# Mamba and attention on four images: another order of work after the last tile of the last image

## The chip, the cores and the metric

The kernel runs on one core of one Trainium2 chip. The metric is the device time of one execution in microseconds (us); lower is better. Three runs of the kernel before gave 7833.92, 7839.31 and 7841.01 us, so the time before is the median, 7839.31 us. All data is float32 unless said.

## What is computed

The input `x` is (4, 512, 64, 64): four images of 512 channels and 4096 positions. Two layers follow each other, each behind a group norm over 16 channels, and each added to its own input:

```python
x = x + L0(_gn(x), ...)
x = x + L1(_gn(x), ...)

# L0: layer norm, a mamba on each of 4 chunks of 128 channels, layer norm, projection
xn = layer_norm(xf, norm_g, norm_b)
ym = mamba(chunks, ...) + skip_scale * chunks      # conv, silu, state scan over 4096 steps
y = einsum('blc,oc->blo', layer_norm(y, norm_g, norm_b), proj_w) + proj_b

# L1: linear attention with 8 heads of 64
q = relu(qkv[:, :, 0]); k = relu(qkv[:, :, 1]); v = qkv[:, :, 2]
kq = einsum('bnhc,bnhd->bhcd', k, q)
attn = einsum('bnhc,bhcd->bnhd', v, kq) / (kq.sum(axis=2) + EPS)
out = attn @ w_out.T + b_out
```

The second group norm needs the whole of an image's L0 output, and `kq` is a sum over all 4096 positions of an image. So the attention of an image can begin only when its last tile has left L0, and the output of L1 only when the whole `kq` is there.

## The kernel before

**Tiles and steps.** An image is cut into 8 tiles of 512 positions (`T`), a tile into 4 chunks of 128 channels. `steps` lists the 128 triples (image, tile, chunk). Each step has 16 slots. A slot scans two blocks of the state (L755, VectorE); ScalarE makes their decay by `Exp` straight into PSUM (L729), GpSimd makes their drive (L737, three buffers tagged `bx`), and every second slot the states are multiplied (VectorE L775 for 384 positions, GpSimd L767 for 128) and folded by TensorE into `y`. The states `h` have two buffers.

**What fills the gaps.** Inside `tc.manual_schedule()` (L1114 to L1202) instructions are issued in the order in which the code calls them. Everything else, the norms of the next tile, `projected` for the tile that has left, and the attention of the image before, is written as generators; `after()` lets them go on by one piece in a slot, `later(n, what)` puts a closure n slots off, `work_bank` takes one of three PSUM banks. `now[0]` is the slot; it is `None` ahead of the loop and behind it, and then nothing waits for a slot and all pieces run at once. Outside the manual part the framework places instructions itself; it may put one of the code behind the loop between instructions of the loop, at a place in its engine's queue where it takes the engine to be free.

**The prologue** (L1089 to L1112): the statistics of image 0, `tile_norm` of its first tile through `group_norm` (L374, ScalarE, four chunks) and `layer_norm` (L435 and L421: VectorE on all four chunks at once; squares at L443, scale at L454 on ScalarE), then the inputs of the first two steps.

**Behind the loop** (L1204 to L1210), for image 3 alone:

- the last chunk's gate and output projection `po`, copied into `xn` (L808);
- `projected` (L517): `layer_scale` sums the channels (`mu_sums`) and squares (L484, `var_sums`), takes mean and variance through two matmuls, and multiplies the tile by the root (L414, L415, L421); then 16 products `pp` with `w_pr`, `xr` by ScalarE (L527), and a GpSimd DMA that adds `x` from DRAM (L545); `shifted` sums values and squares on ScalarE (L575, tiles tagged `res`, two buffers); the tile goes out to DRAM (L548);
- `shifted_end` (L581) and `stats_end` (L344): the group norm's scale `gr` and offset `off` of the whole image;
- `attention` (L822): per 128 positions v, two sums `pq` (q and k) of a bias matmul `bqk` (bf16, L887) and four products with `w_qk`, a `relu` by ScalarE (L848), and 8 small products `pk` for `kq`, summed by VectorE (L855). The tile `xa` is normed on ScalarE (L374). Then `kq` over its norm (`kqn`: memset L912, GpSimd L915 and L919), `m2` (L929) and `m3` (L946), the offsets `pob` (32 products with one column, L967), the identity added to `m3` by GpSimd (L992), and for each tile 16 products `pr` with `m3`, stored by ScalarE and SyncE (L996, L998).

```python
   912          nc.gpsimd.memset(kqn, 0.0)
   ...
   992              nc.gpsimd.tensor_tensor(v, v, fold[r, :].unsqueeze(1).to_broadcast([BLK, NC, BLK]), ALU.add)
```

Of the kernel before, what the change touches and what calls it, by code (L numbers as in the profile page):

```python
# [24 lines left out]
def kernel(  # L25
# [343 lines left out]
    def group_norm(dst, xt, norm):  # L369
        gr, off, _ = norm  # L370
        for c in range(NC):
            if c % 2 == 0:
                yield from clear()
            nc.scalar.activation(  # L374
                dst[:, c, :], xt[:, c, :], AF.Identity,
                bias=off[:, c : c + 1], scale=gr[:, c : c + 1],
            )
            if c == 1:
                yield "free"
        yield  # L380
# [12 lines left out]
    def mean_of(sums, what, when, stop=True):  # L393
# [13 lines left out]
        mm(bank, mean.to_broadcast([P, P]), got, start=True, stop=stop)  # L407
        return bank

    def over_deviation(v, var, name):  # L410
        rs = wk.tile([P, T], F32, tag="sq", name=f"rs_{name}", bufs=4)

        def root():
            nc.scalar.activation(rs, var, AF.Ln, bias=eps)  # L414
            nc.scalar.activation(var, rs, AF.Exp, scale=-0.5)  # L415

        rooted = later(1, root)
        yield
        yield from until(rooted)
        yield "wide"  # L420
        nc.vector.tensor_tensor(v, v, bc(var, NC), ALU.mult)  # L421
        free()
        norming.clear()
        yield

    def layer_norm(v, name):
# [8 lines left out]
        nc.vector.tensor_tensor(v, v, bc(mu, NC), ALU.subtract)  # L435
        free()
        yield "free"
        sqs = []
# [111 lines left out]

    def shifted_stats(b):
# [27 lines left out]
    def shifted_end(f, name):  # L581
        mv = small.tile([P, NC, 2], F32, tag="mv", name=f"mv_{name}", bufs=4)
        for v in range(2):
            nc.vector.tensor_reduce(mv[:, :, v], f[("sum", "square")[v]], AX.X, ALU.add)
        nc.gpsimd.tensor_scalar(mv, mv, 1.0 / L, None, ALU.mult)
        d2 = small.tile([P, NC], F32, tag="d2", name=f"d2_{name}")
        nc.gpsimd.tensor_tensor(d2, mv[:, :, 0], mv[:, :, 0], ALU.mult)
        nc.gpsimd.tensor_tensor(mv[:, :, 1], mv[:, :, 1], d2, ALU.subtract)
        nc.gpsimd.tensor_tensor(mv[:, :, 0], mv[:, :, 0], f["mv"][:, :, 0], ALU.add)
        return mv  # L590


# [229 lines left out]
    def attention(b, x1s, stats):  # L822
# [2 lines left out]
        both = wk.tile([P, NC, C], F32, tag="m3", name=f"kq_{b}", bufs=1)  # L825
        kq = both[:, 0, 0 : C // 2].rearrange("p (c d) -> p c d", c=NC)
        tiles = {}

        def fetch(t, why, spare=1):

# [14 lines left out]
        qk, ready = {}, {}  # L845

        def relu(i, pq):
            nc.scalar.activation(qk[i], pq, AF.Relu)  # L848
            free()

        def add(pk, first):
            if first:
# [24 lines left out]
        for v in range(NT * SUB):  # L877
            t, u = divmod(v, SUB)
            if u == 0:
                gn = yield from fetched(t, "a")  # L880
                yield "free"
                yield from group_norm(gn, gn, norm)
            for j in range(2):
                yield from room()
                i = 2 * v + j
                pq = work_bank(f"pq_{b}_{i}")
                mm(pq, sel[:, 0, j * BLK : j * BLK + 1].to_broadcast([P, P]), bqk, start=True, stop=False)  # L887
                for c in range(NC):
                    mm(
                        pq, gn[:, c, u * P : (u + 1) * P], w_qk[:, c, j * C : (j + 1) * C],  # L890
                        start=False, stop=(c == NC - 1),
                    )
# [19 lines left out]
        nc.gpsimd.memset(kqn, 0.0)  # L912
        nrm = small.tile([P, NC], F32, tag="nrm", name=f"nrm_{b}")
        nc.vector.tensor_reduce(nrm, kq, AX.X, ALU.add)
        nc.gpsimd.tensor_scalar(nrm, nrm, 1e-6, None, ALU.add)  # L915
        nc.vector.reciprocal(nrm, nrm)
        for i in range(P // HEAD):
            r = slice(i * HEAD, (i + 1) * HEAD)
            nc.gpsimd.tensor_tensor(  # L919
                kqn[r, :, r], kq[r, :, :],  # L920
                nrm[r, :].unsqueeze(2).to_broadcast([HEAD, NC, HEAD]), ALU.mult,
            )
# [3 lines left out]
        taken = []  # L926

        def take2(p, pm):
            nc.scalar.copy(m2[:, p, :], pm)  # L929
            free()  # L930

        for p in range(NC):
# [12 lines left out]
        def take3(m, pm):  # L945
            nc.scalar.activation(m3[:, m, :], pm, AF.Copy, scale=gr[:, m : m + 1])  # L946
            free()

        for m in range(NC):
            yield from room()  # L950
# [19 lines left out]
        for o in range(NC):  # L970
            yield from room()
            pm = work_bank(f"pob_{b}_{o}")
            for p in range(NC):
# [11 lines left out]
        yield from until(*taken)  # L985
        free_x()
        free_x()
        for k in range(P // BLK):
# [59 lines left out]
    def leave(b, t):  # L1048
# [4 lines left out]
                for i in range(NT)  # L1053
            ]
        ym = xn[b, t][:, :, NTAP - 1 : NTAP - 1 + T]
        yield from projected(ym, stats1[b], x1s[b][t], b, t)
        if t == NT - 1:
            add_to(rest, attention(b, x1s[b], stats1[b]))

# [204 lines left out]
```

## Time and profile before

| | us |
|---|---|
| median of the runs | 7839.31 |
| the profiled execution | 7841.1 |
| its span, first to last instruction | 7839.4 |
| first scan of the loop starts | 120.77 |
| last scan of the loop ends | 7363.56 |
| first product `pq` of image 3 with `w_qk` | 7426.73 |
| first product `pr` of image 3 | 7722.29 |

| engine | busy us | share of the span |
|---|---|---|
| TensorE (PE) | 6444.4 | 82% |
| VectorE (DVE) | 6905.7 | 88% |
| ScalarE (ACT) | 5461.7 | 70% |
| GpSimd (POOL) | 6898.4 | 88% |

The page gives the busy share of each engine in 40 slices of the span, the chain of work that ended last, and the costliest groups of instructions with what ended the idle time ahead of them. The timeline lists instructions with start and length; equal ones that follow each other are merged ("x8"), and a bracket tells idle time and its releaser. PEld is TensorE's weight load, SPq the queue of SyncE. A float32 matmul stands in the trace as two instructions. All helpers that call `mm` have the line L129, so matmuls are told apart by their tiles. Mean granted TensorE clock: 0.905.

### The profile page before, as it was taken

Reading aid. Unit: us, or ns where it says so; the run is one execution under the profiler, and the core shown is the slowest. Engines: PE = TensorE matmul, PEld = TensorE weight load, DVE = VectorE, ACT = ScalarE, POOL = GpSimd, SP = SyncE. Lnnn points to the kernel's source line nnn. Section 1 sums busy time; section 2 is a strip of 40 time slices with the busy share of each in tenths; the row PEclk is TensorE's granted clock in tenths of the full one; section 3 lists DMA queues with packets and bytes.
Section 4 is the critical chain, followed back from the end, with each engine's and each line's share of the span. In section 5 each row is a group of like instructions: output and inputs, shape, how many; then the busy total and the mean of one; then the engine's idle time right before and its main releaser. Section 6 shows DMA issues by size and latency. Waiting matters only on the chain.

```text
span 7839.4 us, 90421 instructions
## 1 busy us (share of the span) xinstructions
PE 6444.4 (82%) x24839; PEld 2099.0 (27%) x24880; DVE 6905.7 (88%) x5650; ACT 5461.7 (70%) x8329; POOL 6898.4 (88%) x4649
## 2 busy tenths in 40 slices
PE   5677777677789888988788888898788888989599
PEld 1121212112223222322222223332222222323144
DVE  5999999999999999999999999999999999999500
ACT  4677777777777777777777777777777777777421
POOL 4999999999999999999999999999999999999500
PEclk7888878888899999998899999999899999999799
DMA  5666666666666656776666666676666666586302
GB/s 164 165 172 168 158 150 162 162 157 169 174 179 169 159 159 159 192 197 169 174 166 169 167 162 160 171 190 183 164 160 168 157 162 154 148 212 182 100 33 91
DMA packets 829184, 1265.87 MB, mean 161 GB/s; under 512 B 183912, under 2 KB 317560, under 8 KB 816384
## 3 DMA queue, kind: packets, MB, share of 16 engines
q1 hardware_dynamic: 804736, 1222.32, 59.6%
q0 software_dynamic: 16896, 33.56, 2.5%
q8 instruction: 195, 3.19, 0.2%
q10 hardware_dynamic: 7040, 4.20, 0.2%
q14 instruction: 317, 2.60, 0.1%
HBM read 1052.78 MB, written 206.57 MB: 161 GB/s over the span
## 4 chain that ended last, share of the span: by engine, by line
DVE 33%; PE 31%; ACT 10%; issue 8%; DMA 7%; POOL 7%; SPq 3%; POOLq 0%; DVEq 0%; ACTq 0%
DVE h L755 21%; DVE h L775 10%; PE pq L129 6%; PE y L129 6%; PE pc L129 5%; POOL bx L737 5%; ACT dA L729 4%; DMA d_all<-d_rows 3%; PE pr L129 3%; PE po L129 2%; SPq L704 2%; PE pp L129 2%; DMA c_sb<-c_rows 2%; PE pd L129 1%; DMA b_all<-b_rows 1%
## 5 line engine op out<-in xcount | busy, mean ns | idle before, releaser
L737 POOL TENSOR_TENSOR bx<-d_all,b_all 128x1024 f32<-128x1024 f32 x2048 | 4824.0, 2367 | 198.2 <-DVE h L755 178.6
L755 DVE TENSOR_TENSOR_SCAN h<-dA,st,bx 128x512 f32<-128x512 f32 x3584 | 4355.5, 1265 | 292.5 <-PE y L129 101.8
L729 ACT ACTIVATE dA<-d_all,a_t 128x512 f32<-128x512 f32 x4096 | 2759.0, 688 | 1491.5 <-DVE h L755 1434.8
L775 DVE TENSOR_TENSOR h<-h,c_all 128x1536 f32<-128x1536 f32 x1024 | 1768.6, 1727 | 0.1
L767 POOL TENSOR_TENSOR h<-h,c_sb 128x512 f32<-128x512 f32 x1024 | 1299.8, 1269 | 99.1 <-DMA c_sb<-c_rows 13.0
L129 PE MATMUL y<-h,fold 128*32 128x512 f32 x8192 | 1264.0, 693 | 45.7 <-POOL h L767 42.4
L129 PE MATMUL c_all<-parts,sel 128*128 128x384 bf16 x1024 | 369.4, 361 | 1021.9 <-DVE h L775 1020.7
L129 PE MATMUL pc<-xn,w_cv 128*128 128x512 f32 x2048 | 1036.6, 639 | 126.0 <-DVE xn L421 62.2
L129 PE MATMUL pq<-w_qk,xa 128*128 128x512 f32 x2048 | 962.5, 602 | 6.7 <-issue 4.1
L755 DVE TENSOR_TENSOR_SCAN h<-dA,bx 128x512 f32<-128x512 f32 x512 | 590.1, 1204 | 76.6 <-ACT dA L729 46.5
L129 PEld LDWEIGHTS pc<-xn,w_cv 128*128 128x128 f32 x2048 | 386.4, 199 | 735.6 <-issue 409.3
L129 PEld LDWEIGHTS <-sel 128*128 128x128 bf16 x1280 | 126.8, 99 | 1668.0 <-DVE h L775 1453.4
L129 PEld LDWEIGHTS pq<-w_qk,xa 128*128 128x128 f32 x2048 | 395.7, 195 | 437.4 <-issue 421.7
L129 PE MATMUL pp<-xn,w_pr 128*128 128x512 f32 x1024 | 478.0, 597 | 3.8 <-DVE xn L421 3.8
L129 PE MATMUL pr<-xb,m 128*128 128x512 f32 x1024 | 476.1, 603 | 4.8 <-POOL m L992 2.2
L129 PE MATMUL y<-xz,dg 32*32 32x512 f32 x2048 | 362.1, 785 | 0.0
L129 PEld LDWEIGHTS y<-h,fold 128*32 128x32 f32 x8192 | 170.5, 114 | 639.7 <-issue 398.1
L848 ACT ACTIVATE kq<-pq 128x512 f32<-128x512 f32 x256 | 150.8, 589 | 265.5 <-PE pq L129 264.8
L797 POOL TENSOR_TENSOR xz<-xz 128x512 f32<-128x512 f32 x256 | 325.1, 1270 | 10.2 <-ACT xz L794 9.3
L644 POOL TENSOR_TENSOR dt<-dt,xz 128x1024 f32<-128x1024 f32 x128 | 302.1, 2360 | 21.4 <-ACT dt L636 21.4
L855 DVE TENSOR_TENSOR kq<-pk,kq 128x256 f32<-128x256 f32 x124 | 51.2, 413 | 277.9 <-PE pk L129 277.7
L129 PE MATMUL pd<-xz,w_xp 128*128 128x512 f32 x512 | 289.3, 692 | 5.2 <-ACT xz L1066 5.2
(178 smaller groups left out, 6164.7 us busy)
## 6 DMA issues: line engine op xcount, KB each, us to landing
d_all<-d_rows SPq DMA_DIRECT2D x2048, 256.0 KB, 4.3
b_all<-b_rows SPq DMA_DIRECT2D x4096, 64.0 KB, 2.3
d_rows<-dt SPq DMA_DIRECT2D x256, 512.0 KB, 2.7
c_sb<-c_rows SPq DMA_DIRECT2D x4096, 16.0 KB, 3.5
xs<-in_x_dram SPq DMA_DIRECT2D x32, 1024.0 KB, 7.8
xn<-in_x_dram SPq DMA_DIRECT2D x32, 1024.0 KB, 8.4
xr<-in_x_dram POOLq DMA_DIRECT2D x32, 1024.0 KB, 10.2
x<-xr SPq DMA_DIRECT2D x32, 1024.0 KB, 4.5
```

The lines of the kernel that those rows point to most:

```text
L129: nc.tensor.matmul(out_, lhsT, rhs, **how)
L644: nc.gpsimd.tensor_tensor(f["both"][:, 1], f["both"][:, 0], f["xz"][:, 0], ALU.mult)
L704: nc.sync.dma_start(dst[k * BLK : (k + 1) * BLK, :], rows_[q * KS + k, :].partition_broadcast(BLK))
L729: nc.scalar.activation(dAs[k], fs[n]["d_all", e][:, 0, j, :], AF.Exp, scale=a_t[:, e, j, q : q + 1])
L737: nc.gpsimd.tensor_tensor(bxs[g], fs[n]["d_all", e][:, 1, jj * 2 : jj * 2 + 2, :], bc(b_all[g // JJ], 2), ALU.mult)
L755: nc.vector.tensor_tensor_scan(h[:, j, :], dAs.pop(2 * g + i), bxs[g][:, i, :], 0.0 if t == 0 else st[:, c, e, q, j : j + 1], ALU.mult, AL ...
L767: nc.gpsimd.tensor_tensor(h[:, :, CUT:], h[:, :, CUT:], bc(c_sb.pop(g // JJ), NJ), ALU.mult)
L775: nc.vector.tensor_tensor(own, own, bc(c_all.pop(g // JJ), NJ), ALU.mult)
L797: nc.gpsimd.tensor_tensor(f["xz"][:, 1, e, :], f["xz"][:, 1, e, :], f["xz"][:, 0, e, :], ALU.mult)
L848: nc.scalar.activation(qk[i], pq, AF.Relu)
L855: nc.vector.tensor_tensor(kq, pk, kq, ALU.add)
```

## The change

Line numbers in this section are those of the diff's own code; L-numbers elsewhere are of the kernel before. Where `now[0]` is `None` (prologue and end) or the image is the last:

- `group_norm` does every second chunk on VectorE; `over` does the two layer norm operations of VectorE chunk by chunk instead of in one instruction.
- `projected_last` takes the place of `projected` for the last tile: the products `pp` are made of the tile before its norm, chunk by chunk into four banks of their own, and VectorE multiplies them by the root `rs` behind; `x` is loaded early by SyncE and added by VectorE; the statistics come from `bn_stats`.
- the small operations of `shifted_end` and of `kqn` go from GpSimd to VectorE.
- the last attention adds the q/k bias on VectorE to the sum in PSUM, with the bias loaded over all partitions into a `bx` buffer, and ScalarE then does `Relu` in place; the bias matmul goes.
- `m2` is copied by ScalarE and VectorE in turn; the identity is added by VectorE in 16 blocks as `m3` comes; `pob` is taken in four banks, first all products with `m2`, then those with `m3` (which has its identity by then, so `ngm` is taken off `bo` first).

```diff
@@ group_norm
+            if now[0] is None and c % 2:
+                nc.vector.tensor_scalar(
+                    dst[:, c, :], xt[:, c, :], gr[:, c : c + 1], off[:, c : c + 1], ALU.mult, ALU.add
+                )
+            else:
+                nc.scalar.activation(
+                    dst[:, c, :], xt[:, c, :], AF.Identity,
+                    bias=off[:, c : c + 1], scale=gr[:, c : c + 1],
+                )
...
+    def over(v, m, op):
+        if now[0] is None:
+            for c in range(NC):
+                nc.vector.tensor_tensor(v[:, c, :], v[:, c, :], m, op)
+        else:
+            nc.vector.tensor_tensor(v, v, bc(m, NC), op)
...
+    def projected_last(ym, f, x1, b, t):
+        nm = f"{b}_{t}"
+        xt = load_now(cols(x, b)[:, :, t * T : (t + 1) * T], f"xr_{nm}")
+        sq = wk.tile([P, NC, T], F32, tag="h", name=f"sq_{nm}", bufs=2)
+        sums, squares = work_bank(f"mu_sums_{nm}"), work_bank(f"var_sums_{nm}")
+        for c in range(NC):
+            nc.scalar.activation(sq[:, c, :], ym[:, c, :], AF.Square, bias=about)
+            sums_into(sums, {c: ym[:, c, :]}, (c,))
+            sums_into(squares, {c: sq[:, c, :]}, (c,))
+        got = {}
+        for what, bank in (("mu", sums), ("var", squares)):
+            got[what] = wk.tile([P, T], F32, tag="sq", name=f"got_{what}_{nm}", bufs=4)
+            nc.scalar.copy(got[what], bank)
+        mu = work_bank(f"mu_{nm}")
+        mm(mu, mean.to_broadcast([P, P]), got["mu"], start=True, stop=True)
+        mu2 = wk.tile([P, T], F32, tag="sq", name=f"mu2_{nm}", bufs=4)
+        nc.scalar.activation(mu2, mu, AF.Square, bias=about)
+        var = work_bank(f"var_{nm}")
+        mm(var, mean.to_broadcast([P, P]), got["var"], start=True, stop=False)
+        mm(var, minus_first.to_broadcast([P, P]), mu2, start=False, stop=True)
+        rs = wk.tile([P, T], F32, tag="sq", name=f"rs_{nm}", bufs=4)
+        nc.scalar.activation(rs, var, AF.Ln, bias=eps)
+        nc.scalar.activation(rs, rs, AF.Exp, scale=-0.5)
+        last = small.tile([P, NC, 1, 6], F32, tag="first", name=f"last_{nm}")
+        pps = [spare_bank(f"pp_{nm}_{o}", o) for o in range(NC)]
+        for c in range(NC):
+            for o in range(NC):
+                mm(
+                    pps[o], w_pr[:, c, o * P : (o + 1) * P], ym[:, c, :],
+                    start=(c == 0), stop=(c == NC - 1),
+                )
+        for o in range(NC):
+            nc.vector.tensor_tensor(sq[:, o, :], pps[o], rs, ALU.mult)
+            nc.vector.scalar_tensor_tensor(
+                xt[:, o, :], sq[:, o, :], pb[:, o : o + 1], xt[:, o, :], ALU.add, ALU.add
+            )
+            nc.vector.bn_stats(last[:, o, 0, :], xt[:, o, :])
+        nc.sync.dma_start(x1, xt)
+        mv = aggregate(last, f"last_{nm}")
...
+    def spare_bank(name, i):
+        if i < LEAD:
+            return ps_d.tile([P, T], F32, tag="dA", name=name)
+        return ps_y.tile([P, T], F32, tag="y", name=name)
...
@@ attention
+        last = b == B - 1
+        if last:
+            bias = wk.tile([P, 2, C], F32, tag="bx", name=f"bias_{b}", bufs=3)
+            nc.sync.dma_start(
+                bias.rearrange("p j c -> p (j c)"), b_qkv[0 : 2 * C].partition_broadcast(P)
+            )
...
         def relu(i, pq):
+            if last:
+                nc.vector.tensor_tensor(qk[i], pq, bias[:, i % 2, :], ALU.add)
+                free()
+                nc.scalar.activation(qk[i], qk[i], AF.Relu)
...
-                mm(pq, sel[:, 0, j * BLK : j * BLK + 1].to_broadcast([P, P]), bqk, start=True, stop=False)
+                if not last:
+                    mm(
+                        pq, sel[:, 0, j * BLK : j * BLK + 1].to_broadcast([P, P]), bqk,
+                        start=True, stop=False,
+                    )
...
         def take2(p, pm):
-            nc.scalar.copy(m2[:, p, :], pm)
+            if last and p % 2:
+                nc.vector.tensor_copy(m2[:, p, :], pm)
+            else:
+                nc.scalar.copy(m2[:, p, :], pm)
...
+            if last:
+                for k in range(P // BLK):
+                    r = slice(k * BLK, (k + 1) * BLK)
+                    v = m3[r, m, m * P + k * BLK : m * P + (k + 1) * BLK]
+                    nc.vector.tensor_tensor(v, v, fold[r, :], ALU.add)
...
+        if last:
+            banks = [spare_bank(f"pob_{b}_{o}", o) for o in range(NC)]
+            nc.vector.tensor_tensor(bo, bo, ngm, ALU.subtract)
+            for v, rhs in ((m2, bv), (m3, ngm)):
+                for o in range(NC):
+                    for p in range(NC):
+                        mm(
+                            banks[o][:, 0:1], v[:, p, o * P : (o + 1) * P], rhs[:, p : p + 1],
+                            start=(v is m2 and p == 0), stop=(v is m3 and p == NC - 1),
+                        )
...
-        yield from projected(ym, stats1[b], x1s[b][t], b, t)
+        do = projected_last if now[0] is None else projected
+        yield from do(ym, stats1[b], x1s[b][t], b, t)
```

More of the change, by code (lines that the diff above doesn't have):

```diff
@@ L373, in group_norm @@
                 yield from clear()
[L374 to L377, printed above, removed]
+            if now[0] is None and c % 2:
[7 more added lines that the diff above has]
+                )
             if c == 1:
@@ L420, in over_deviation @@
         yield "wide"
-        nc.vector.tensor_tensor(v, v, bc(var, NC), ALU.mult)
+        over(v, var, ALU.mult)
         free()
@@ L434, in layer_norm @@
         yield "wide"
-        nc.vector.tensor_tensor(v, v, bc(mu, NC), ALU.subtract)
+        over(v, mu, ALU.subtract)
         free()
@@ L549, in projected @@
         later(2, free_x)
+    def projected_last(ym, f, x1, b, t):
[37 more added lines that the diff above has]
+        mv = aggregate(last, f"last_{nm}")
+        d = mv[:, :, 0]
+        nc.vector.tensor_tensor(d, d, f["mv"][:, :, 0], ALU.subtract)
+        nc.vector.tensor_scalar(f["sum"][:, :, t], d, float(T), None, ALU.mult)
+        nc.vector.tensor_tensor(d, d, d, ALU.mult)
+        nc.vector.tensor_tensor(d, d, mv[:, :, 1], ALU.add)
+        nc.vector.tensor_scalar(f["square"][:, :, t], d, float(T), None, ALU.mult)
+        free_x()
+        yield
@@ L584, in shifted_end @@
             nc.vector.tensor_reduce(mv[:, :, v], f[("sum", "square")[v]], AX.X, ALU.add)
-        nc.gpsimd.tensor_scalar(mv, mv, 1.0 / L, None, ALU.mult)
+        eng = nc.vector if now[0] is None else nc.gpsimd
+        eng.tensor_scalar(mv, mv, 1.0 / L, None, ALU.mult)
         d2 = small.tile([P, NC], F32, tag="d2", name=f"d2_{name}")
-        nc.gpsimd.tensor_tensor(d2, mv[:, :, 0], mv[:, :, 0], ALU.mult)
-        nc.gpsimd.tensor_tensor(mv[:, :, 1], mv[:, :, 1], d2, ALU.subtract)
-        nc.gpsimd.tensor_tensor(mv[:, :, 0], mv[:, :, 0], f["mv"][:, :, 0], ALU.add)
+        eng.tensor_tensor(d2, mv[:, :, 0], mv[:, :, 0], ALU.mult)
+        eng.tensor_tensor(mv[:, :, 1], mv[:, :, 1], d2, ALU.subtract)
+        eng.tensor_tensor(mv[:, :, 0], mv[:, :, 0], f["mv"][:, :, 0], ALU.add)
         return mv
@@ L847, in relu @@
         def relu(i, pq):
-            nc.scalar.activation(qk[i], pq, AF.Relu)
-            free()
+            if last:
[3 more added lines that the diff above has]
+            else:
+                nc.scalar.activation(qk[i], pq, AF.Relu)
+                free()
         def add(pk, first):
@@ L890, in attention @@
                         pq, gn[:, c, u * P : (u + 1) * P], w_qk[:, c, j * C : (j + 1) * C],
-                        start=False, stop=(c == NC - 1),
+                        start=(last and c == 0), stop=(c == NC - 1),
                     )
@@ L914, in attention @@
         nc.vector.tensor_reduce(nrm, kq, AX.X, ALU.add)
-        nc.gpsimd.tensor_scalar(nrm, nrm, 1e-6, None, ALU.add)
+        eng = nc.vector if last else nc.gpsimd
+        eng.tensor_scalar(nrm, nrm, 1e-6, None, ALU.add)
         nc.vector.reciprocal(nrm, nrm)
@@ L918, in attention @@
             r = slice(i * HEAD, (i + 1) * HEAD)
-            nc.gpsimd.tensor_tensor(
+            eng.tensor_tensor(
                 kqn[r, :, r], kq[r, :, :],
@@ L928, in take2 @@
         def take2(p, pm):
-            nc.scalar.copy(m2[:, p, :], pm)
+            if last and p % 2:
+                nc.vector.tensor_copy(m2[:, p, :], pm)
+            else:
+                nc.scalar.copy(m2[:, p, :], pm)
             free()
@@ L968, in offset @@
             free()
-        for o in range(NC):
+        if last:
[8 more added lines that the diff above has]
+                        )
+            for o in range(NC):
+                offset(o, banks[o])
+        for o in range(0 if last else NC):
             yield from room()
@@ L987, in attention @@
         free_x()
-        for k in range(P // BLK):
+        for k in range(0 if last else P // BLK):
             r = slice(k * BLK, (k + 1) * BLK)
```

## The prediction

> **What bounds the kernel now.** I read the slices of the page first, then the chain of waits and the windows behind the loop, then the timeline at the places that the change touches.
>
> ```profile
> PE   5677777677789888988788888898788888989599
> ...
> DVE  5999999999999999999999999999999999999500
> ...
> POOL 4999999999999999999999999999999999999500
> ```
>
> Two regimes: up to slice 37 VectorE and GpSimd are both full; in the last three slices they are at rest and TensorE is full. The loop ends at 7363.56 us, so the end of image 3 is 476 us, 6% of the span. A wait or an instruction there is on the path unless TensorE covers it.
>
> ```profile
> 7406.63 8.36 DMA xr<-in_x_dram
> ...
> 7426.73 12.82 PE pq L129 x24
> ...
> 7688.85 20.04 PE pm L129 x40
> ...
> 7708.89 11.24 PE pob L129 x64
> ...
> 7722.29 113.10 PE pr L129 x256
> ```
>
> This is the chain in order of time: a serial head until 7426.73, then TensorE without a break but for a hand-over at 7684.5 and another at 7720.
>
> ```profile
> 7443.76 0.38 PE L129 MATMUL pq<-bqk,sel 128*128 128x512 bf16 x1
> ...
> 7443.98 3.60 PE L129 MATMUL pq<-w_qk,xa 128*128 128x512 f32 x8
> ```
>
> The bias matmul starts 0.22 us ahead of the next: its price on a full TensorE.
>
> ```profile
> 7277.15 0.19 POOL L766 COPY st<-h 128x4 f32<-128x4 f32 x1
> ...
> 7278.64 4.68 POOL L737 TENSOR_TENSOR bx<-d_all,b_all 128x1024 f32<-128x1024 f32 x2
> ...
> 7281.05 1.28 DVE L755 TENSOR_TENSOR_SCAN h<-dA,st,bx 128x512 f32<-128x512 f32 x1 [0.53 <-ACT sum L575]
> ...
> 7281.07 0.72 ACT L575 ACTIVATE square<-xr,moff 128x512 f32<-128x512 f32 x1
> ...
> 7420.17 0.52 POOL L912 MEMSET kqn<- 128x512 f32 x1 [12.23 <-ACT sum L575]
> ```
>
> These are taken from two stretches of the timeline. In the first GpSimd is never idle, and its first `bx` of that pair (7278.64 to 7281.01) is ready just as the scan at 7281.05 takes it: no lead at all. The last line shows the memset of `kqn`, waiting for a buffer of tag `res`.
>
> **The Trainium skill.** (1) "TensorE: Matmul & The Clock Gate", part 1: the array runs at half clock until about 3.4 us of unbroken work, and falls back after as long a rest. The windows agree: granted clock 0.51 from 7376.0 to 7383.6, 0.99 from 7393.5 to 7405.2; a float32 product of 512 columns takes 1.71 or 0.86 us. (2) Same page, back-to-back issue gap: N / 2.4 GHz + 2.5 ns, 216 ns for 512 columns; measured 0.22 us. (3) Same page, the queue-depth row: ScalarE, VectorE and GpSimd are strict FIFO. The memset above, 12.23 us idle ahead of it, is what a blocked queue looks like. (4) "VectorE: DVE Perf Modes", walkthrough: a float32 tensor_tensor makes one element per cycle at 0.96 GHz, a tensor_scalar in SBUF two. Here 413 ns for 256 elements (L855), 682 for 512 (L321), 481 for a tensor_scalar of 512 (L315).
>
> **The parts.** Times are on the clock of the profile before.
>
> *Prologue.* Chunks overlap now. Norm: ScalarE's last of four ends at 59.6; two on each engine end at 58.15, and the sums of the channels follow: -1.4. Mean: 2.29 us in one instruction and then four squares end 4.5 us after the start; in chunks (0.60 us pitch, squares 0.62) 3.4: -1.1. Root: the first product `pc` needs chunk 0 alone; 2.29 + 0.73 becomes 0.69 + 0.73: -1.6. Together -4.1. The sums' burst is shorter, so the small matmul behind it, at full clock before (1.12 us), may fall to half (2.07, as at 70.56): +0.6 taken. Everything to the first scan at 120.77 hangs on this chain. Sum -3.5, between -2.0 and -4.1.
>
> *The loop.* The built order of instructions is the same on VectorE, ScalarE (bar three squares behind its last decay) and SyncE (bar one early load, whose buffer is long free). On GpSimd one row moves: the memset of `kqn` now stands inside the loop, between the copy at 7277.15 and L767 at 7277.42. The buffer that it takes is freed by the last square of tile 6 (7281.07 to 7281.79, its accumulator read to 7281.9). So GpSimd stands still until 7281.9; memset 0.52, L767 1.27, first `bx` 2.36: ready at 7286.1 for a scan that came at 7281.05. Queued behind the memset are L767, both `bx` and the next copies; VectorE's scans wait for them. GpSimd has no idle time until 7326, VectorE's later stalls wait for folds that hang on its own products, so nothing is made up: +5.1. Bounds: 0, were the lead larger, and 5.9, all of the stall. Not below zero, as nothing is taken from the loop. The memset's place at 7420.17 lay beside other work, so moving it gains nothing.
>
> *Head, 7363.56 to 7426.73.* Before: `po` ends 7371.6, sums, mean, squares, variance, root, norm to 7389.4, 16 products to 7405.2, `x` 8.36 us, ScalarE's statistics to 7420.8, then 4.6 from `pm` to `pq`. After: sums and squares of chunks 0 to 2 and four of the 16 products go ahead of or between the steps of chunk 3. TensorE works unbroken from 7365.57; full clock took 4.4 us from 7389.43, so I take it from 7370.5.
> - Last fold 7367.5; `var_sums` of three chunks 1.9, `pp_1` 1.4: 7370.8. `po`'s second product, which would have started at 7369.54, stands behind these: 7371.8. ScalarE copies `xn`, 7372.4.
> - `pp_2`, `mu_sums`, `pp_3`, `var_sums` of chunk 3 at 0.86 each: 7375.2; two copies 7375.9; `pp_0`, mean and variance 7377.6; ScalarE's square of the mean 0.69 and the last term: 7378.7. Root `rs` 7380.1.
> - 11 products left: 7388.0; bank 0 is full at 7385.5. `rs` is not late.
> - VectorE: three operations per bank (multiply from PSUM, add of `pb` and `x`, bn_stats: nearest rows 682, 682, 677 ns, 0.60 pitch) x 4 = 7.2 from 7385.6, aggregates 0.3: 7393.1. 11 small ones at 0.19: 7395.5. Then 4.6 as before, and 0.2 for the new operation on `bo`: first `pq` 7400.3.
>
> Gain 26.4; I take -26.0. At half clock throughout it is near -18; with full clock at once near -28. The old DMA of 8.36 us goes; the new load of `x` lands long before 7385.6. `xa_2` can load only after the last store (7392.7 + 4.5 + 7.6 = 7404.8), and its norms stand ahead of the second bias add on VectorE; the first `pq` sum lasts to about 7406, so this is covered by 1 us, and 6 us before TensorE needs it.
>
> *q and k.* 64 bias matmuls go. Three of them lay in the wait of `pm` (7422.6 to 7424.6): nothing. 61 x 0.22 = -13.4. Put in: per sum a VectorE add from PSUM (between 413 ns for half the size and 0.69; 0.69 taken) and a `Relu` from SBUF (0.60 as from PSUM). Both lie beside TensorE: `pk` of one v comes after a further `pq` of 3.43 us, and the two need 1.4 with hops. Bounds: -7.3, if `pk`'s neighbour then shows its weight load (0.19 x 32), to -14.
>
> *Hand-over at 7684.5.* The add is on the path, +0.7; GpSimd's two `kqn` products (0.61 each) and `nrm` become VectorE's (0.34 pitch, from 413 ns at this size): -0.7. Sum 0, +-0.5. The split copies of `m2` gain nothing: the products run without a gap from 7688.85, and a copy is due only when its chunk's turn comes.
>
> *End.* `pob` has its 32 products as before. The identity's four GpSimd steps and their hops, 7720.13 to 7722.29, go beside `m3`'s products on VectorE (16 small ones, four after the last, while 16 `pob` products with `m2` keep TensorE busy): -2.2, between -1 and -3.
>
> Sum: -3.5 + 5.1 - 26.0 - 13.4 + 0 - 2.2 = -40.0. The profiled execution took 7841.1, so 7801.1; it lies 1.8 above the median of the runs, 7839.31, against which the forecast is 7799.3.
>
> **Rivals.**
> - *No stall in the loop* (the square comes earlier, or GpSimd's lead is larger than this one execution shows): 7799.3 - 5.1 = 7794.2. Against it stands the row at 7281.05. Chance 0.20.
> - *TensorE stays cold in the head*, since the short waits between its steps don't count as work: head -18, 7807. For it: clock 0.50 and 0.51 up to 7383.6 before, with 5.1 of 7.15 us busy. Chance 0.13.
> - *The bias matmul hid a weight load*: q and k -7.3, 7805.4. For it: the "issue" pieces of 0.16 us beside `pk`. Chance 0.07.
> - *VectorE's queue is blocked by a norm that waits for its tile* (slower): the two norms of `xa_3` stand in its queue ahead of the add of `pq_9`, and so of `pk_4`. The load may start when tile 0 is done and lands 7.6 us later; `pk_4` needs the add 2.4 us after that, and norms, add and `Relu` take about 2.3. Five tiles are in this place. Each us of lateness then stops TensorE for 1 us: at 16 us per load the whole gain is gone (40 / 5 = 8 beyond the 7.7), beyond 20 us it is slower by over 0.2%, say 7860. Against it: DMA share 0.09 in this stage, and 3.4 us in all that ScalarE waited for these loads before. Chance 0.05: 0.03 within 0.2%, 0.02 slower.
> - *The forecast*, 0.55: 7799.3, by itself 7794 to 7805.
>
> **The numbers.** 0.2% is 15.7 us, about what a measurement of this kernel tells from no change. All cases but the blocked queue gain over 32 us: faster 0.93, with 0.02 for several failures at once within 0.2%, same 0.05, slower 0.02. The range takes in the no-stall case with the better bounds of the head and the prologue, and the cold head: 7790 to 7811.
>
> **What would show it.** Right: first scan near 117; a GpSimd gap of about 4.7 us ahead of the memset inside the loop, some 84 us ahead of the last scan, and last scan near 7365 (-3.5 + 5.1); 37 us from the last scan to the first `pq`; 7.58 us per v; 2 us from `pob` to `pr` gone. Wrong: full clock later than 5 us into the head; TensorE idle between `pq` and `pk`; a last scan earlier than 7362.

## The result, and the profile after

The changed kernel takes 7797.76 us (median of 6 runs, 7791.69 to 7819.03), the kernel before 7840.16 us (6 runs, 7833.92 to 7846.71). The ratio is 0.9948, with a 95% interval of 0.9937 to 0.9959, so the gain of 0.5% is clear of the noise. The forecast was 7799.3 us.

The profiled executions can be set side by side in six stretches, cut at events that both traces have. Scans are counted from 0; scan 4040 is the eighth ahead of the place where the memset now stands. The six add up to the two spans, 7839.39 and 7797.01 us.

| stretch, us | before | after | difference | predicted |
|---|---|---|---|---|
| start to first scan | 120.77 | 116.95 | -3.82 | -3.5 |
| first scan to scan 4040 | 7146.06 | 7141.50 | -4.56 | 0 |
| scan 4040 to the end of the last scan | 96.73 | 102.76 | +6.03 | +5.1 |
| last scan to first `pq` | 63.17 | 35.53 | -27.64 | -26.0 |
| first `pq` to first `pm` (q, k, hand-over) | 262.12 | 252.50 | -9.62 | -13.4 |
| first `pm` to the end | 150.54 | 147.77 | -2.77 | -2.2 |
| sum | | | -42.38 | -40.0 |

The slices of the page of the changed kernel:

```profile
PE   5677777677789888987788889898788888899699
...
DVE  5999999999999999999999999999999999999720
...
POOL 4999999999999999999999999999999999999700
```

The loop is as full as it was. VectorE's last three slices show 7, 2, 0 where they showed 5, 0, 0: it now works beside TensorE in the end of image 3. TensorE is full in the last slices as before.

The timeline of the changed kernel around the memset, where the prediction expected a stop (start, length, engine, line; in brackets the idle time ahead and what ended it):

```profile
7268.70 0.20 POOL L835 COPY st<-h 128x4 f32<-128x4 f32 x1
...
7272.66 0.72 ACT L643 ACTIVATE square<-xr,moff 128x512 f32<-128x512 f32 x1
...
7273.53 0.53 POOL L996 MEMSET kqn<- 128x512 f32 x1 [4.63 <-ACT square L643]
...
7275.23 4.66 POOL L806 TENSOR_TENSOR bx<-d_all,b_all 128x1024 f32<-128x1024 f32 x2
...
7277.62 1.28 DVE L824 TENSOR_TENSOR_SCAN h<-dA,st,bx 128x512 f32<-128x512 f32 x1 [5.52 <-POOL bx L806]
```

This answers to the lines of GpSimd shown of before. Where the copy was followed 0.27 us later by L767, GpSimd now waits 4.63 us for the last square of tile 6, clears `kqn`, and only then makes the `bx` that VectorE's next scan needs. VectorE stands still for 5.52 us; before it was 0.53.

The chain of waits of the changed kernel in the head, in order of time (start, length, engine, tile, line):

```profile
7375.13 6.88 PE pp L129 x16
7382.13 0.70 DVE sq L599
...
7389.32 0.58 DVE last L603
7389.90 0.23 DVE mv_last L341 x2
...
7394.51 1.05 POOL gr_b L364
...
7396.74 3.78 PE pq L129 x4
```

The DMA of 8.36 us and ScalarE's sums are gone from it. VectorE's work on the four banks, 7.8 us from 7382.13 to 7389.90, has taken their place. The rest of the chain of the changed kernel:

```profile
7649.24 20.25 PE pm L129 x40
7669.48 9.30 PE pob L129 x56
7682.20 110.92 PE pr L129 x254
```

`pr` no longer waits for GpSimd behind `pob`; two of its instructions lie inside `pob` already, as the timeline of TensorE shows:

```profile
7678.65 2.06 PE L129 MATMUL pr<-xb,m 128*128 128x512 f32 x2
7680.49 1.71 PE L129 MATMUL pob<-ngm_b,m 128*128 128x1 f32 x8
```

In the q and k stage of the changed kernel (timeline of TensorE) there is no bias matmul between the sums:

```profile
7410.02 0.69 PE L129 MATMUL pk<-kq 128*64 128x64 f32 x16
7410.64 7.13 PE L129 MATMUL pq<-w_qk,xa 128*128 128x512 f32 x16
7417.70 0.69 PE L129 MATMUL pk<-kq 128*64 128x64 f32 x16
```

From one `pk` to the next it is 7.68 us, not 8.02 as before and not 7.58 as predicted.

The clock in the head is the last thing to compare. The figures of the kernel before, and then those of the changed one, between the same two times (busy time and number of instructions by engine, then the granted clock, the share of the DMA engines and GB/s):

```profile
7364.00:7382.00 18.00, 11.66 (x22) 2.14 (x22) 1.43 (x1) 4.99 (x8) 2.42 (x2) 0.50 0.00 0
```

```profile
7364.00:7382.00 18.00, 17.87 (x47) 6.43 (x41) 0.00 (x0) 5.07 (x8) 1.26 (x1) 1.00 0.00 0
```

Before, TensorE executed 22 matmul instructions here at half clock, with a third of the time idle; now 47 at full clock, almost without a gap.

### The profile page after: what moved, and what is told of

It reads as the page before. It is cut to its first block, busy times and chain, and to the rows that moved or that the text cites. A ratio compares the mean times of both kernels' runs of the same rounds, so it can differ in the third digit from the quotient of the medians.

```text
span 7797.0 us, 90419 instructions
## 1 busy us (share of the span) xinstructions
PE 6424.5 (82%) x24816; PEld 2092.9 (27%) x24816; DVE 6968.4 (89%) x5784; ACT 5442.5 (70%) x8289; POOL 6892.5 (88%) x4637
## 4 chain that ended last, share of the span: by engine, by line
DVE 34%; PE 30%; ACT 10%; DMA 9%; issue 8%; POOL 6%; SPq 3%; DVEq 0%; POOLq 0%; ACTq 0%
DVE h L824 21%; DVE h L844 10%; PE y L129 6%; PE pc L129 6%; PE pq L129 5%; POOL bx L806 5%; DMA d_all<-d_rows 4%; ACT dA L798 3%; PE pr L129 3%; PE po L129 3%; SPq L773 3%; DMA c_sb<-c_rows 2%; PE pp L129 2%; DVE xn L421 2%; PE c_all L129 1%
## 5 line engine op out<-in xcount | busy, mean ns | idle before, releaser
L129 PE MATMUL pz<-xn,w_z 128*128 128x512 f32 x512 | 270.5, 621 | 7.5 <-ACT xz L692 6.0
L129 PE MATMUL po<-xz,w_op 128*128 128x512 f32 x512 | 258.8, 628 | 5.2 <-POOL xz L866 5.0
```

The source lines that it names most:

```text
L129: nc.tensor.matmul(out_, lhsT, rhs, **how)
```

## The experiments

Three questions were open: whether the memset is what costs 6 us and the 4.6 us gained ahead of it are chance; which parts the head's gain comes from and what bounds it now; and where 0.10 us per v went in the q and k stage. Below, "scan 4040 to the end" is the sum of the last four stretches of the table: 572.56 us before, 538.56 after. by_bank, pairs, q_kept, x_alone, k_kept and warm_end were executed once each (7789.57 to 7830.76 us); beside the chance of the loop, which is measured below, such a time tells nothing of edits this small, and only the stretches of their traces are used.

### The changed kernel again, and with the memset elsewhere

The changed kernel without an edit (after_again):

> The changed kernel once more, for the spread of the loop between executions. Theory (the 4.6 us that the loop had gained ahead of the memset are chance of its transfers): the last 128 scans take 224.7 us again within 0.2, while the scans ahead of them, 7019.5 us in the changed kernel and 7024.1 in the one before, move by several us. Rival (the change itself makes the loop faster): 7019.5 within 1 us.

The memset elsewhere (memset_late):

> The changed kernel with one edit: for the last image kqn takes a buffer of tag bx instead of tag res, so that its memset stands at the end of the loop in GpSimd's queue. Theory (the memset stops the loop): no stall of 4.96 us at that scan; the last 128 scans take 218.7 us as in the kernel before, not 224.7; ratio to the kernel before 0.9940, some 6 us below the changed kernel. Rival (the loop has slack and gives the stall back: it became only 1.5 us longer in all): the last 128 scans are shorter, but the time stays that of the changed kernel, 0.9948.

```diff
-        kqn = wk.tile([P, NC, P], F32, tag="res", name=f"kqn_{b}", bufs=2)
+        if last:
+            kqn = wk.tile([P, 2, C], F32, tag="bx", name=f"kqn_{b}", bufs=3)[:, 0, :]
+            kqn = kqn.rearrange("p (c d) -> p c d", c=NC)
+        else:
+            kqn = wk.tile([P, NC, P], F32, tag="res", name=f"kqn_{b}", bufs=2)
```

The changed kernel again: 7808.47 us (7796.14 to 7811.02), ratio 0.9961 (0.9948 to 0.9973). Its last 128 scans took 224.76 us (first time 224.75), the scans ahead of them 7016.63 us (first time 7019.51): the end repeats to 0.01 us, the rest does not. With the memset elsewhere: 7796.33 us (7793.07 to 7798.56), ratio 0.9948 (0.9936 to 0.9961). The 0.9940 that was expected is not reached, and the time alone decides nothing, since the two intervals overlap. The traces do. From scan 4040 on, the timeline of the kernel with the memset elsewhere:

```profile
7275.94 4.67 POOL L806 TENSOR_TENSOR bx<-d_all,b_all 128x1024 f32<-128x1024 f32 x2
...
7278.34 1.28 DVE L824 TENSOR_TENSOR_SCAN h<-dA,st,bx 128x512 f32<-128x512 f32 x1 [0.49 <-POOL bx L806]
...
7358.52 0.52 POOL L1000 MEMSET kqn<- 128x512 f32 x1 [2.19 <-DVE h L824]
7360.88 0.19 POOL L835 COPY st<-h 128x4 f32<-128x4 f32 x1 [1.83 <-DVE h L824]
```

The same scan waits 0.49 us instead of 5.52. The memset stands behind the last `bx`, with 1.83 us to spare ahead of the next instruction of GpSimd. Scan 4040 to the last scan takes 96.54 us against 102.76 and 102.73: the memset costs 6.2 us, and the loop gives none of it back. Scan 4040 to the end is 531.64 us, 6.9 less than in the changed kernel; behind the loop the two differ with the clock, which is taken up below. The last 128 scans did not come down to 218.7 but to 220.22; the remaining 1.5 us lie ahead of scan 4040.

All fourteen profiled executions of this study together settle the other half. The order of VectorE's instructions up to scan 4040 is the same in all. First scan to scan 4040 takes between 7138.20 and 7153.85 us, and kernels with the memset inside the loop lie at both ends of that. The mean is 7144.7 us for the nine with it and 7144.5 for the five without. So the 4.56 us in the table are chance. Scan 4040 to the last scan, in contrast, takes 96.5 to 96.7 us in the five kernels without the memset there and 101.6 to 103.3 in the nine with it.

### One part alone on the kernel before

The new end of the last tile (head_alone):

> The kernel before with the new end of the last tile alone (projected_last and the small operations of shifted_end on VectorE). Theory (this part both gains the head and frees the res buffer that lets the memset into the loop): last scan to first pq 35.5 to 37 us instead of 63.2, memset inside the loop with a stall of 5 us and 224.7 us for the last 128 scans, 8.02 us per v as before; -27 + 6 = -21 us, ratio 0.9973. Rival (the memset comes into the loop through another part): last 128 scans 218.7, ratio 0.9965.

```diff
+    def projected_last(ym, f, x1, b, t):
...
-        nc.gpsimd.tensor_scalar(mv, mv, 1.0 / L, None, ALU.mult)
+        eng = nc.vector if now[0] is None else nc.gpsimd
+        eng.tensor_scalar(mv, mv, 1.0 / L, None, ALU.mult)
...
-        yield from projected(ym, stats1[b], x1s[b][t], b, t)
+        do = projected_last if now[0] is None else projected
+        yield from do(ym, stats1[b], x1s[b][t], b, t)
```

7813.17 us (7805.47 to 7825.26, 7 runs), ratio 0.9970 (0.9959 to 0.9981). Last scan to first `pq` is 35.53 us, to the hundredth that of the changed kernel, the stage of q and k keeps its 8.02 us per v, and the memset stands inside the loop: 103.28 us from scan 4040 to the last scan. One part brings the whole gain of the head and the whole stall.

`x` and the statistics of the last tile by VectorE, without the new order (x_alone):

> The kernel before with the second half of the head alone: x loaded early by SyncE and added by VectorE, bn_stats; the norm stays ahead of the projection. Theory (the two halves of the head add up: 18 us by the order of norm and products and by the clock, 9 to 13 by x and the statistics): last scan to last product pp 41.6 us as before, from there to the first pq about 8.5 instead of 21.6; together 50. The clock is 0.5 up to the first pp as before. Rival (the warm clock comes with any change that keeps the tail shorter): last scan to last pp shorter than 39.

```diff
-        xt = new_tile(f"xr_{nm}")
+        last = now[0] is None
+        if last:
+            xt = load_now(cols(x, b)[:, :, t * T : (t + 1) * T], f"xr_{nm}")
+            st = small.tile([P, NC, 1, 6], F32, tag="first", name=f"last_{nm}")
+        else:
+            xt = new_tile(f"xr_{nm}")
...
         def take(o, pp):
+            if last:
+                nc.vector.scalar_tensor_tensor(
+                    xt[:, o, :], pp, pb[:, o : o + 1], xt[:, o, :], ALU.add, ALU.add
+                )
+                free()
+                nc.vector.bn_stats(st[:, o, 0, :], xt[:, o, :])
+                return
```

(Behind the last product it goes on with the small operations of `projected_last`.) Last scan to last `pp` is 43.34 us (41.56 before; the clock rose 4.2 us later), from there to the first `pq` 8.46 (21.61 before): the second half did what was expected of it, 13.1 us. The clock was lower than in the changed kernel: 0.72 on the mean of the stretch from 7376.0 us to the last `pp`. So the head's 27.6 us in the changed kernel are two things: 18.2 up to the last `pp` (41.56 to 23.36), by the new order and the clock that comes with it, and 9.4 behind it (21.61 to 12.17). The second number is 3.7 us short of what the same part gives alone, because all four banks now fill at the same moment. Here too the memset lies in the loop (103.19 us). What x_alone and head_alone share, and qk_alone below lacks, is that the statistics of the last tile no longer take buffers of tag `res`; that the memset waits for that tag is what memset_late showed.

### The products of the last tile bank by bank

The order of the 16 products (by_bank):

> The changed kernel with the products pp of the last tile taken bank by bank (o outside, c inside) instead of chunk by chunk. Theory (VectorE's twelve operations on the banks are the path from the last product on, since all four banks fill at the very end): bank 0 is full when the root is there, VectorE's work ends 3.3 us earlier, last scan to first pq 32.2 us instead of 35.5. Rival (TensorE's small matmuls, ScalarE or the load of xa set the start of pq): 35.5.

```diff
-        for c in range(NC):
-            for o in range(NC):
+        for o in range(NC):
+            for c in range(NC):
```

Last scan to first `pq` is 32.44 us, 3.1 less (32.2 were expected). VectorE in the timeline of this kernel:

```profile
7382.45 0.69 DVE L599 TENSOR_TENSOR sq<-pp,rs 128x512 f32<-128x512 f32 x1 [13.53 <-ACT rs L589]
...
7387.02 0.69 DVE L599 TENSOR_TENSOR sq<-pp,rs 128x512 f32<-128x512 f32 x1 [0.30 <-PE pp L129]
...
7390.46 0.69 DVE L599 TENSOR_TENSOR sq<-pp,rs 128x512 f32<-128x512 f32 x1 [1.01 <-PE pp L129]
...
7391.97 0.69 DVE L603 BATCH_NORM_STATS2 last<-xr 128x6 f32<-128x512 f32 x1
```

The first bank waits for the root now, no longer for products, and the last two wait for TensorE. Only the last bank's three operations lie behind the last product. VectorE was indeed the path behind the products.

### The offset of q and k, and the weight load behind pk

The offset of q and k (qk_alone):

> The kernel before with the q and k offset on VectorE alone, the bias matmul gone. Theory (the bias matmul hid 0.10 us of a weight load behind every pk): 7.68 us per v, first pq to last pk 250.2 instead of 259.2; ratio 0.9988. Rival (the 0.10 us come from another part of the change): 7.58 us per v, 247; ratio 0.9984. In both no memset inside the loop.

```diff
+        last = b == B - 1
...
-            nc.scalar.activation(qk[i], pq, AF.Relu)
-            free()
+            if last:
+                nc.vector.tensor_tensor(qk[i], pq, bias[:, i % 2, :], ALU.add)
+                free()
+                nc.scalar.activation(qk[i], qk[i], AF.Relu)
...
-                mm(pq, sel[:, 0, j * BLK : j * BLK + 1].to_broadcast([P, P]), bqk, start=True, stop=False)
+                if not last:
+                    mm(
```

7826.71 us (7814.57 to 7838.47, 20 runs), ratio 0.9984 (0.9978 to 0.9991), which cannot tell 0.9984 from 0.9988. The trace can: 7.68 us per v, first `pq` to last `pk` 249.50 us. The missing 0.10 us come with this part, and the memset does not lie in the stretch behind scan 4040 (96.59 us).

The bias matmul of q kept (q_kept):

> The changed kernel with the bias matmul kept for q (the sum that follows a pk) and removed for k. Theory (behind a pk the bias matmul hides 0.105 us of the weight load): 7.80 us per v, that is 7.68 + 0.23 - 0.105. Rival (it hides nothing): 7.90, that is 7.68 + 0.22.

```diff
-            if last:
+            if last and i % 2:
                 nc.vector.tensor_tensor(qk[i], pq, bias[:, i % 2, :], ALU.add)
...
-                if not last:
+                if not last or j == 0:
                     mm(
```

7.89 us per v. That seemed to speak against the theory, until the timeline showed that the edit had kept the one of the two that does not stand behind a `pk`:

```profile
7428.84 0.69 PE L129 MATMUL pk<-kq 128*64 128x64 f32 x16
7429.46 3.70 PE L129 MATMUL pq<-w_qk,xa 128*128 128x512 f32 x8
7432.99 0.38 PE L129 MATMUL pq<-bqk,sel 128*128 128x512 bf16 x1
7433.21 3.60 PE L129 MATMUL pq<-w_qk,xa 128*128 128x512 f32 x8
```

Behind `pk` comes the sum of k, and q's bias matmul stands between two sums. The eight instructions behind `pk` take 3.70 us, those behind the bias matmul 3.60. The other one was kept next:

The bias matmul of k kept (k_kept):

> The changed kernel with the bias matmul kept for k and removed for q. In q_kept the sum of q was not the one behind a pk, as its expectation had it: the trace of it shows pk ahead of the sum of k, with 0.70 us for the product behind it as in the changed kernel, and the bias matmul at its full 0.22 us elsewhere (7.89 us per v). Theory (a weight load shows behind a pk, and the bias matmul hid it there): 7.80 us per v. Rival (the bias matmul hid nothing anywhere): 7.89 again.

```diff
-            if last:
+            if last and i % 2 == 0:
                 nc.vector.tensor_tensor(qk[i], pq, bias[:, i % 2, :], ALU.add)
...
-                if not last:
+                if not last or j == 1:
                     mm(
```

7.80 us per v, as the theory had it:

```profile
7422.43 0.69 PE L129 MATMUL pk<-kq 128*64 128x64 f32 x16
7423.04 0.39 PE L129 MATMUL pq<-bqk,sel 128*128 128x512 bf16 x1
7423.27 7.03 PE L129 MATMUL pq<-w_qk,xa 128*128 128x512 f32 x16
```

With the bias matmul between, the 16 instructions take 7.03 us instead of 7.13. So the one bias matmul was worth 0.21 us (7.89 - 7.68) and the other 0.12 (7.80 - 7.68), together 0.33 of the 0.34 that were measured.

The timeline agrees with a weight load that shows. Here is the end of a `pk` in the changed kernel, and then in the kernel before:

```profile
7418.31 0.19 PEld L129 LDWEIGHTS pq<-w_qk,xa 128*128 128x128 f32 x1
7418.31 0.70 PE L129 MATMUL pq<-w_qk,xa 128*128 128x512 f32 x1
```

```profile
7656.64 0.10 PEld L129 LDWEIGHTS <-sel 128*128 128x128 bf16 x1
7656.64 0.39 PE L129 MATMUL pq<-bqk,sel 128*128 128x512 bf16 x1
```

The load of the first product behind a `pk` starts with the product; within a sum it starts 0.43 us ahead, under the product before. With a load of 0.19 us beside it the product takes 0.70 us instead of 0.59. The bias matmul has a load of 0.10 us beside it there and takes 0.39 instead of 0.38, and the load of the next product lies under it.

Two `pk` in a row (pairs):

> The changed kernel with the pk of two v taken one behind the other, so that a sum pq follows a pk half as often. Theory (each time a product of 512 columns follows the short pk products, 0.105 us of its weight load shows): 15.26 us per two v instead of 15.36. Rival (the 0.105 us belong to each pk, or to VectorE's and ScalarE's work on q and k): 15.36 per two v.

```diff
-                qk[i] = both[:, 1 + i % 3, :]
+                qk[i] = both[:, 1 + i % 3, :]
+                if last:
+                    qk[i] = more[:, i % 7 - 3, :] if i % 7 > 2 else both[:, 1 + i % 7, :]
...
-                if v and j == 0:
+                if last and v and v % 2 == 0 and j == 0:
+                    yield from sums(v - 2)
+                    yield from sums(v - 1)
+                elif not last and v and j == 0:
                     yield from sums(v - 1)
```

(`more` is a buffer of tag `h`, free by then.) 15.02 us per two v: 0.34 less, three times what was expected. I had priced one side of the change of shape only.

```profile
7440.55 0.69 PE L129 MATMUL pk<-qk 128*64 128x64 f32 x16
7441.06 0.64 PE L129 MATMUL pk<-kq,qk 128*64 128x64 f32 x16
7441.63 5.85 PE L129 MATMUL pq<-w_qk,xa 128*128 128x512 f32 x13
```

A `pk` by itself costs 0.81 us of TensorE: its first product starts 0.52 us behind the last one of `pq` instead of 0.43, `pq` follows 0.62 us later, and that sum's first product takes 0.53 instead of 0.43. Two in a row cost 0.09 + 0.51 + 0.57 + 0.10 = 1.27 us. The difference, 2 x 0.81 - 1.27 = 0.35, agrees with the 0.34 measured. From the first `pm` to the end this kernel also took 143.35 us instead of 147.77, which nobody had expected; see below.

### Short products and the clock at the end

`pob` between the products of `m3` (warm_end):

> The changed kernel with the 16 pob products of m2 put between the four groups of m3's products instead of behind them. Theory (the run of short pob products lets the clock fall to 0.50, and the first pr products pay for it): a clock of 0.9 or more behind the last pm and in the first 4 us of pr, and 2 to 4 us less from the last pm to the last pr (123.6 in the changed kernel). Rival (the clock falls whatever the order, since the one-column products themselves are at fault or the wait ahead of pm is): 123 to 124.

```diff
         for m in range(NC):
+            if last and m:
+                pob(m2, bv, m - 1)
...
-            for v, rhs in ((m2, bv), (m3, ngm)):
-                for o in range(NC):
...
+            pob(m2, bv, NC - 1)
+            for o in range(NC):
+                pob(m3, ngm, o)
```

(`pob(v, rhs, o)` is the old loop over p for one bank.) The last `pm` to the last `pr` fell by 5.9 us (123.62 to 117.69), but that counts in the `pob` products that now stand ahead of that `pm`. First `pm` to the end, which does not, is 144.55 us, 3.2 less. The other half of the theory failed: the clock in the first 4 us of `pr` was 0.50 as before, and `pr` took 114.34 us against 114.46. So the gain is that 12 of the 32 `pob` products ran at full clock among those of `m3`; that `pr` pays for `pob` with its first microseconds was not removed. The stretch of half clock around `pob` and the start of `pr` lasted 6.8 us instead of 13.7.

### The versions put together

memset_late, by_bank and pairs in one kernel (best):

> The changed kernel with the edits of memset_late, by_bank and pairs together. Theory (the three act in different stretches and add up): 96.6 us from scan 4040 to the last scan instead of 102.8, last scan to first pq 32.4, 7.51 us per v; scan 4040 to the end 538.6 - 6.2 - 3.1 - 8.5 = 521; ratio to the kernel before about 0.9926 with the loop's chance of several us on top. Rival (one of them takes what another gives, such as a clock that falls elsewhere): over 526.

7784.27 us (7780.46 to 7791.75), ratio 0.9930 (0.9916 to 0.9943), against 0.9948 (0.9937 to 0.9959) of the changed kernel: the intervals overlap by 0.0006. Scan 4040 to the end is 520.69 us, where 521 was expected and 538.56 measured for the changed kernel. The sum adds up, its terms do so less well: last scan to first `pq` took 33.89 us instead of 32.4, since the clock rose later, and first `pq` to first `pm` 245.20 us against 246.57 in pairs.

warm_end on top of that (best2):

> The edits of best and of warm_end together. Theory (pob's products run at full clock between those of m3, whatever the clock ahead of pm): 520.7 - 3.2 = 517.5 us from scan 4040 to the end, ratio to the kernel before 0.9926 in comparison with 0.993 for best. Rival (in best the clock is already up behind the last pm, 0.92 against 0.71, so that there is less to gain): 519 to 520.7.

7786.74 us (7782.09 to 7789.98), ratio 0.9936 (0.9922 to 0.9949); scan 4040 to the end 520.78 us. The rival holds: first `pm` to the end is 145.06 us in both, and the stretch of half clock around `pob` lasts 10.2 us in both, so this order of `pob` had nothing left to gain there.

## Why the prediction was right

The sum was right to 2.4 us of 42, better than its terms, and that is luck: the loop's chance (-4.6) and what the clock happened to give in the head and at the end (-1.7 and about -1.5) set off what was missed in q and k (+3.8), in the stall (+0.9) and at the end (+0.9). The mechanisms of the three large terms, the stall, the head and the bias matmuls, were as stated; the last of them was mis-sized.

Of its signs of being right, the first scan (116.95 us for 117), GpSimd's gap (4.63 for 4.7), the head (35.5 for 37) and the missing 2 us between `pob` and `pr` came true; 7.58 us per v did not (7.68). One of its signs of being wrong came true as well: the last scan ended at 7361.21 us, earlier than 7362. The cause is the loop's chance of 4.56 us, not a missing stall.

- *Prologue*, -3.5 predicted, -3.82 measured, by other pieces. First norm to the first `pc` takes 17.21 us instead of 20.54, -3.3 for the -3.5 of the working. From `pc` to the first scan it was 2.1 shorter, and the norm itself began 1.6 later in this execution. Neither was in the sum. The 2.1 are not settled: the ten executions with the new prologue took 41.3 to 41.8 us for it and three of the four with the old one 43.6, but the fourth (head_alone) took 40.2. The -3.82 are one pair of executions. The first scan came at 119.0 to 122.2 us in the four with the old prologue and at 113.8 to 118.4 in the ten with the new one, means 120.4 and 115.9. No run has this part alone.
- *Loop*, +5.1 predicted, +6.03 measured, with the mechanism as stated: memset, 4.63 us of idle GpSimd (4.7 predicted), VectorE late by as much. The stall itself added 4.96 us; two later waits, for a fold and for GpSimd's state product, grew by 0.44 and 0.64. That nothing would be made up was right. That nothing would be added was the small error, and 5.9 was too low as an upper bound. The rival without a stall is refuted by both traces and by memset_late.
- *Head*, -26.0 predicted, -27.64 measured. The root came 15.3 us behind the last scan (16.5 predicted), the last product ended at 23.4 (24.4), `pq` began at 35.5 (36.7). (One sum of that working is off: 7393.1 and 11 x 0.19 make 7395.2, not 7395.5.) The difference is the clock: full not from 7370.5, 6.9 us behind the last scan, but from 0.2 us behind it. The first `pp` and `var_sums` stand ahead of the fold and kept TensorE at work there, but the same order did not always bring this: in memset_late, k_kept, best and best2 the clock rose 5.9 to 6.3 us behind the last scan, nearly as assumed, and memset_late then took 37.18 us to the first `pq`, where the prediction's sum gives 37.2. So the head was priced rightly, and the 1.7 us more are luck with the clock (see below). The rival of a TensorE that stays cold throughout fails in all eleven executions with the new order.
- *q and k with the hand-over*, -13.4 predicted, -9.62 measured. Here the rival of the hidden weight load was half right. The step that failed is "61 x 0.22": for the bias matmuls of k it is 0.12, not 0.22, because each stood behind a `pk` and covered 0.10 us of a load. Over 30 intervals that makes -10.2. The first v took 0.53 us more at half clock. The bound of -7.3 had the whole load of 0.19 us come to light; 0.105 of it did. At the hand-over the wait for the last `pk` grew by 0.76 us, for the add, and the wait ahead of `pm` shrank by 0.56. The added operations cost what was taken for them (691 ns for the add, 630 for the `Relu`) and nothing on the path before that. TensorE did not stand still between `pq` and `pk` until the last v, and VectorE's norms waited for their loads 2.6 us in all, so that the blocked queue did not come about.
- *End*, -2.2 predicted, -2.77 measured, which by itself proves little: kernels whose end is that of before took 146.83 to 150.54 us for it, with the clock. Executions whose clock changed at the same times behind the first `pm`, to 0.1 us, can be compared: 149.14 us with the old end (head_alone) and 147.84 with the new (q_kept); 147.91 (x_alone) and 146.62 (memset_late). So the end is worth 1.3 us, not 2.2, and the rest of the 2.77 is the clock. The 2.17 us between `pob` and `pr` are gone, but they were priced as if at full clock, while `pr` then starts earlier in a stretch of half clock, where they are worth about half (estimate: 2.17 / 2 = 1.1).

The Trainium skill, "TensorE: Matmul & The Clock Gate", part 1, says that the window that watches the activity runs freely and doesn't begin with the work. The traces agree: in each of the fourteen all changes of the granted clock, about 400 in an execution and always from 0.50 to 1.00 or back, lie on one grid of 3.413 us, to 1 ns, from the first to the last. What matters is how work and rests fall on that grid. Here are pieces of it around the last scan, first in the changed kernel, then in memset_late (length, busy time and instructions of five engines, TensorE first; then the granted clock and two figures of the DMA):

```profile
7357.99:7361.40 3.41, 3.41 (x11) 0.70 (x10) 3.31 (x4) 1.19 (x2) 0.12 (x1) 0.50 0.74 300
7361.40:7364.82 3.42, 2.03 (x15) 0.49 (x14) 1.67 (x1) 1.24 (x3) 1.34 (x2) 1.00 0.00 0
```

```profile
7356.84:7360.25 3.41, 2.92 (x10) 0.81 (x11) 3.41 (x4) 0.44 (x1) 0.52 (x1) 0.50 0.94 333
7360.25:7363.66 3.41, 2.29 (x7) 0.25 (x9) 2.31 (x2) 1.50 (x3) 1.46 (x2) 0.50 0.06 24
7363.66:7367.07 3.41, 3.41 (x15) 0.92 (x8) 0.00 (x0) 0.59 (x1) 1.26 (x1) 0.50 0.00 0
7367.07:7370.49 3.42, 3.42 (x9) 0.93 (x7) 0.00 (x0) 1.31 (x2) 0.00 (x0) 1.00 0.00 0
```

Both times the clock is full from the piece that follows one filled by TensorE. In the changed kernel a piece ends just behind the work ahead of the fold and is full; in memset_late that work lies across two.

It is the same with the rests ahead of `pm`. In pairs and in best TensorE rests 0.90 and 2.28 us alike. In pairs they fell into two pieces, 1.41 us in one and 1.77 in the other, and the clock of the 4 us behind was 1.00; in best one piece had 2.48 us, and it was 0.57. In the kernel before and in x_alone, with rests of 0.75 and 2.89 us alike, it was 0.50 and 0.64, for pieces that began at different places. In all fourteen executions half clock followed a piece there with 2.06 us of rest or more, and never one with 1.77 or less. That is less than the rest of about 3.4 us that the prediction took from that page; the measurement decides. It also explains why pairs gained 4.4 us behind `pm`, and best, with the same order, 2.7: the difference of 1.7 us is what one piece of 3.41 us at half clock costs.

## What to carry to other kernels

When an edit frees a buffer, look at what will take that buffer next and where the scheduler then puts the instruction that waits for it: one harmless memset, moved some 150 us up a full queue, cost 6 us, and another tag mends it. Before costing a small matmul at its pitch, look at its neighbours, since a change of shape between short and long products costs time that the small one may cover. And when a loop varies by 15 us between executions, cut the traces at common events and compare the stretches, not the sums. For stretches behind a rest of TensorE, compare executions whose clock changed at the same times: a part that seemed to gain 2.8 us gained 1.3.

## What was not expected of the hardware

- A group of 16 short float32 instructions (64 columns) between long ones costs 0.81 us where two groups in a row cost 0.64 each: 0.09 us are lost on entering the first and 0.10 on leaving the last.
- The same loop, in the same order, took 7138 to 7154 us to scan 4040, while its last 96 us repeat to 0.2 us when nothing blocks.
- With equal rests ahead of it, a stretch of matmuls may begin at full or at half clock, by where the rests fall on the grid of 3.413 us; kernels with the same end took 146.83 to 150.54 us for it.
